# First window steps of the second block written beside the second batch's combine, in shared PSUM pairs and handed-on SBUF places

## The chip, the cores and the metric

The kernel runs on one core of one Trainium2 chip. The metric is device time in microseconds (us) of one execution. Engines are named as in the profile: PE (TensorE), with its weight loads as PEld, DVE (VectorE), ACT (ScalarE), POOL (GpSimd) and SP (SyncE, which here only issues DMAs).

## What is computed

Two batches of 1024 tokens with 256 features pass two blocks. Everything is fp32. Cut to what matters:

```python
x = x + soft_mixture(attention(x))      # block 0
x = x + layers(quaternion_rotation(x))  # block 1, two layers

def soft_mixture(x):                    # 64 experts of 32 slots
    logits = einsum('bmd,dnp->bmnp', x, phi)
    dispatch = softmax(logits, axis=0)                       # over the batch
    combine = softmax(logits.reshape(b, m, n * p), axis=-1)  # over 2048 slots
    slots = einsum('bmd,bmnp->bnpd', x, dispatch)
    y = einsum('bnpd,nde->bnpe', slots, W) + bias
    return einsum('bnpd,bmnp->bmd', y, combine)

def layer(x):
    h = shift_token(x)                  # second half of the features: one token back
    q, k, v = heads(h @ wqkv)           # 8 heads of 64
    q, k = rotary(l2norm(q) * qs, l2norm(k) * ks)
    x = x + local_attention(q, k, v) @ wo   # windows of 128, each sees itself and the one before
    a, g = split(layernorm(shift_token(x)) @ w1 + b1)
    return x + (a * gelu(g)) @ w2 + b2
```

The quaternion rotation is one 256x256 matrix (`rot`), applied to every token.

## The kernel before, in words

Five stages follow each other. **Attention** (lines 140 to 730) works on (batch, group of four heads) units. **The mixture's logits, dispatch and experts** (`logits`, `dispatch`, `experts`, lines 749 to 815) run over 32 iterations `it`: four quarters of the slots, eight pairs of token tiles in each (tile m of both batches). `logits` writes the raw logits to DRAM, one tensor `lgd[i]` of 128 tokens x 2048 slots for each of 16 token tiles; `experts(g0)` makes 8 experts' outputs and adds the bias into `y`. **The combine** (lines 819 to 887) reads those rows back. `weigh(i)` loads row i by one DMA of 1 MB into one of five places, takes its maximum (DVE, line 824), its exp and sum (ACT, 827) and scales it by 1/sum (POOL, 829). `turn(q, jj)` transposes a quarter of the slots of a pair of rows on PE (837) and copies the result from PSUM, on DVE for odd jj (844), on ACT for even (846). `combine(q, jj)` multiplies it with `y` (856); the four quarters of one q gather in one PSUM pair, and the last one adds them to the tokens `xT` on DVE (867). q = 0 to 3 are batch 0, q = 4 to 7 batch 1. `rotate(h)` (879) applies `rot` to half a batch: it fills `xa` through ACT and stores the tokens in DRAM (`xkeep`) for the end. The loop at line 966 writes, for each of 32 parts (q, jj), the turn of the next part and the combine of this one; rotations 0, 1 and 2 stand within it, rotation 3 behind it. Then `psum.close()` gives back all PSUM.

**The window stage** (lines 991 to 1384) covers both layers' attention and feed-forward. Its loop counts steps s from -2 on; window i is 128 tokens, windows 0 to 7 are batch 0 of the first layer, 8 to 15 batch 1. In step s stand the projection and rotation of window s + 2 (`project`, `rotate_parts`, `values`, `norms`, `rotated`), the turn into head-major form of window s + 1, the scores, maxima, exps and divisions of window s in two halves of four heads (`scores` 1122, `maxima` 1139, `weights` 1156, `divide` 1172), the transposed weights of window s - 1 (`turn_e` 1183) and its mix with the values (`mix` 1202). After each fourth window comes `project_out` (1222). The feed-forward follows eight steps later, by `forward(s - 8)`: `centre`, `normalise`, six `gate`s and a `feed` for each 512 tokens, so from s = 6 on.

`rotate_parts` reads the projection's PSUM twice, by ACT (`raw`, 1047) and by DVE (`t1`, 1055); POOL multiplies `raw` with the other table (1057). `norms` is a DVE sum of squares (1066) and twelve small POOL operations (1073 to 1076). The first half of heads is divided on POOL, the second on DVE.

**What sets the order.** Tile makes the semaphores: an instruction waits for the last writers and readers of what it touches. In the window stage PE, DVE, ACT and POOL run in exactly the written order (`manual_schedule`), and each engine's queue is strict: what stands behind a waiting instruction waits too. In the combine's stage only PE's order is written out, and a scheduler orders the rest. SP's order is the scheduler's in both.

**Places.** [...] Before the window stage they are two pools of two pairs (`wide`, `pair`); in it three pairs in a ring (`two_banks`, line 1008) and two single banks (`bank`). A tile in a ring waits for the readers of the tile that held its place. In SBUF the combine's rows, `eT` and `y` lie in pools `mo` and `mo2`; `lw` holds the second block's weights, masks and tables; `la` the window stage's tiles; `fa` the feed-forward's. The weights of the second block's first layer are all loaded before the combine's loop (line 965).

Of the kernel before, what the change touches and what calls it, by code (L numbers as in the profile page):

```python
# [17 lines left out]
P = 128  # L18
# [73 lines left out]
def tile_kernel(ctx: ExitStack, tc: tile.TileContext, a: dict, out: bass.AP):  # L92
# [7 lines left out]
    ones_v = const.tile([P, P], F32, name="ones_v")  # L100
    nc.vector.memset(ones_v, 1.0)
# [22 lines left out]
    wts = ctx.enter_context(ExitStack())  # L124
    with tc.tile_pool(name="xin", bufs=1) as xin, tc.tile_pool(name="l0", bufs=1) as l0, ExitStack() as right:
        xT = xin.tile([P, 2, T], F32, name="xT")

        def load_x(engine, t0, n):
            engine.dma_start(xT[:, :, t0 : t0 + n], a["xT"][:, t0 : t0 + n].rearrange("(c p) t -> p c t", p=P))

        load_x(nc.sync, 0, 512)
        load_x(nc.sync, 512, 512)
        gcoh = l0.tile([P, T // P, H0], F32, name="gcoh")
        fac = l0.tile([P, T // P], F32, name="fac")
# [5 lines left out]
        psum = ExitStack()  # L140
        ps_s = psum.enter_context(tc.tile_pool(name="ps_s", bufs=2, space=PSUM))
        ps_t = psum.enter_context(tc.tile_pool(name="ps_t", bufs=2, space=PSUM))
        at = ExitStack()
        at1 = at.enter_context(tc.tile_pool(name="at", bufs=1))
        at2 = at.enter_context(tc.tile_pool(name="at2", bufs=2))
        w_att = at1.tile([P, 2, N_ATT], F32, name="w_att")
        at0 = {n: W_ATT[n].start for n in W_ATT}
        for engine, lo, n in (
            (nc.scalar, at0["wq"], P),
            (nc.scalar, at0["wk"], P),  # L150
            (nc.scalar, at0["wv"], D),
            (nc.sync, at0["wq"] + P, P),
            (nc.sync, at0["wk"] + P, P),
            (nc.sync, at0["wout"], D),
        ):
            engine.dma_start(
                w_att[:, :, lo : lo + n], a["w_att"][:, lo : lo + n].rearrange("(c p) n -> p c n", p=P)
            )
        mxt = [at1.tile([P, 4, 4, 32], F32, name=f"mxt{i}") for i in range(2)]
        for t in mxt:  # L160
            nc.gpsimd.memset(t, 0.0)

        VW = HD0 + 1
        v = [at1.tile([P, 8, H0 * VW + 32 - VW], F32, name=f"v{b}") for b in range(B)]
        for t in v:
            nc.gpsimd.memset(t, 1.0)
        sv = [at1.tile([P, D], F32, name=f"sv{b}") for b in range(B)]

        def watt(name, c, lo, n):
            at = W_ATT[name].start + lo  # L170
            return w_att[:, c, at : at + n]

        def wide(name):
            return ps_s.tile([P, 2, 512], F32, tag="s", name=name)

        def pair(name):
            return ps_t.tile([P, 2, 512], F32, tag="t", name=name)

        pvs = {}

        def values(b, half, tile, part):

            if part == 0:
                pvs[b, half] = tile("pv").rearrange("p x (y d) -> p (x y) d", d=D)
            pt = pvs[b, half]
            for y in (2 * part, 2 * part + 1):
                j = 4 * half + y
                for k in range(2):
                    nc.tensor.matmul(
                        pt[:, y, :],  # L190
                        xT[:, k, b * S + j * P : b * S + (j + 1) * P],
                        watt("wv", k, 0, D),
                        start=(k == 0),
                        stop=(k == 1),
                    )
            if part == 0:
                return
            nc.vector.tensor_tensor(
                v[b][:, 4 * half : 4 * half + 4, 0 : H0 * VW].rearrange("p j (h d) -> p j h d", d=VW)[
                    :, :, :, 0:HD0  # L200
                ],
                pt.rearrange("p j (h d) -> p j h d", d=HD0),
                bcast(rows[:, ROWS["bv"]].rearrange("p (h d) -> p h d", d=HD0), 1, 4),
                ALU.add,
            )

        def token_sums(b, k):

            if k == 0:
                xws[b] = at2.tile([P, 2], F32, tag="xsum", name="xsum")  # L210
            nc.vector.tensor_reduce(xws[b][:, k : k + 1], xT[:, k, b * S : (b + 1) * S], AX.X, ALU.add)

        def value_sums(b, tile):

            pt = tile("psv")
            for k in range(2):
                nc.tensor.matmul(
                    pt[:, 0, :D],
                    xws[b][:, k : k + 1].to_broadcast([P, P]),
                    watt("wv", k, 0, D),  # L220
                    start=(k == 0),
                    stop=(k == 1),
                )
            nc.vector.scalar_tensor_tensor(
                sv[b], rows[:, ROWS["bv"]], float(S), pt[:, 0, :D], ALU.mult, ALU.add
            )

        units = [(b, g) for b in range(B) for g in range(4)]
        mxs, obs, o_tms, oTs, xws, heads = {}, {}, {}, {}, {}, {}
# [3 lines left out]
        qm = [at1.tile([P, S], F32, name=f"qm{i}") for i in range(2)]  # L233
        qs = [at1.tile([P, S], F32, name=f"qs{i}") for i in range(2)]
        km = [at1.tile([P, S], F32, name=f"km{i}") for i in range(3)]
        for i in (0, 1, 2):
            nc.vector.memset(km[i], 0.0)
            nc.vector.tensor_scalar(km[i], km[i], col("kaug"), None, ALU.add)
            if i < 2:
                nc.vector.memset(qm[i], 0.0)  # L240

        def project_in(b, what, c, tile):

            pt = tile("pqk")
            for n in range(2):
                project_part(pt, b, what, c, n)
            project_end(pt, what, c)

        def project_part(pt, b, what, c, n):
            t0 = b * S + n * 512  # L250
            for k in range(2):
                nc.tensor.matmul(  # L252
                    pt[:, n, :],
                    watt(f"w{what}", k, c * P, P),
                    xT[:, k, t0 : t0 + 512],
                    start=(k == 0),
                    stop=(k == 1),
                )

        def project_end(pt, what, c):  # L260
            heads[what] = at1.tile([P, S], F32, tag=f"h{what}", name=f"h{what}")
            nc.scalar.activation(
                heads[what], pt.rearrange("p n t -> p (n t)"), AF.Identity, bias=col(f"b{what}", c)
            )

        def spread(u):

# [5 lines left out]
        def maxima(step, half):  # L273
# [3 lines left out]
            if hu not in mxs:  # L277
                mxs[hu] = at2.tile([P, 4, 4, 2], F32, tag="mx2", name=f"mx2_{hu}")
# [145 lines left out]
        with tc.tile_pool(name="pro", bufs=1, side="right") as pro:  # L424
# [68 lines left out]
            def coherence_in(b, n, c):  # L493
# [12 lines left out]
                if c == 0:  # L506
                    return
# [995 lines left out]
```

## Time and profile before

| | |
|---|---|
| median of 3 runs | 1725.86 us (1725.84 to 1725.88) |
| the profiled execution | 1725.92 us |
| its span, first to last instruction | 1724.1 us |
| TensorE's clock, mean granted | 0.989 |
| combine, batch 0 / batch 1 | about 804 to 887 / 887 to 967 us |
| window steps s = -2 to 7 | 967 to 1115 us |

The span and 1.8 us around it make the execution. A line of busy time gives the sum of an engine's instructions; matmuls are pipelined and their ends modelled, so two neighbours overlap a little, and the distance of two starts is the better measure of what one costs. The granted clock is a share of full speed. A row of waits names the waiting instruction, what released it, the us in total, how many, and the longest. A stretch's row has one pair of busy time and count for each engine in the order PE, PEld, DVE, ACT, POOL, then the granted clock, the DMA engines' busy share and GB/s.

### The profile page before, as it was taken

To read this page: it belongs to the slowest core of one execution; us is meant where nothing else is said; L and a number is where in the kernel's file an instruction comes from. 1 tells how busy PE (TensorE), PEld (TensorE's weight loads), DVE (VectorE), ACT (ScalarE), POOL (GpSimd) and SP (SyncE) were. 2 spreads that over 40 slices of the span, in tenths; PEclk is the share of its full clock that TensorE was granted. 3 is DMA by queue.
4 is the path that set the end of the run, shared out by engine and by line. 5 is a ranking of instruction groups with operands and counts; after the bars stand their busy time and mean duration, and the time that the engine had idled before them with its cause. 6 is when DMAs were issued, how large, how long until landed. Compare 5 with 4: busy or idle time off the path is not lost.

```text
span 1724.1 us, 22245 instructions
## 1 busy us (share of the span) xinstructions
PE 1670.0 (97%) x8684; PEld 847.2 (49%) x8684; DVE 930.1 (54%) x1599; ACT 834.3 (48%) x1331; POOL 518.4 (30%) x732
## 2 busy tenths in 40 slices
PE   8999999999999999999999878999999999999998
PEld 4333443343433444445788545545555555555543
DVE  5767767766772222233443366666565656575522
ACT  1456556655667222244332254556565656565520
POOL 2101101111110100023563355555464534455301
PEclk9999999999999999999999988999999999999999
DMA  5100000010000434554731000000100000000000
GB/s 148 50 13 13 1 13 13 1 19 7 1 1 13 135 122 134 158 196 156 278 144 65 13 0 1 1 1 0 62 1 13 1 1 34 17 1 25 1 25 36
DMA packets 41881, 82.55 MB, mean 48 GB/s; under 512 B 3708, under 2 KB 24016, under 8 KB 39216
## 3 DMA queue, kind: packets, MB, share of 16 engines
q1 hardware_dynamic: 39232, 75.29, 13.3%
q0 software_dynamic: 1584, 5.29, 1.1%
q8 instruction: 68, 1.11, 0.3%
q10 hardware_dynamic: 960, 0.56, 0.1%
q14 instruction: 37, 0.30, 0.1%
HBM read 55.95 MB, written 20.97 MB: 45 GB/s over the span
## 4 chain that ended last, share of the span: by engine, by line
PE 87%; DVE 4%; POOL 4%; ACT 3%; issue 1%; DMA 1%; DVEq 0%; ACTq 0%; POOLq 0%
PE sc L314 9%; PE pga L1268 8%; PE po L333 7%; PE lg L755 6%; PE cmb L856 6%; PE sl L781 6%; PE pm L282 6%; PE py L1291 5%; PE pq L1033 4%; PE pwo L1222 3%; PE pv L1089 3%; PE sc L1122 3%; PE pe L1183 3%; PE po L1202 3%; ACT e L322 2%; PE pqk L252 2%
## 5 line engine op out<-in xcount | busy, mean ns | idle before, releaser
L289 DVE TENSOR_REDUCE mx<-pm 128x2 f32<-128x1024 f32 x256 | 304.5, 1220 | 86.6 <-PE pm L282 82.6
L322 ACT ACTIVATE e<-sc 128x1024 f32<-128x1024 f32 x256 | 254.0, 1023 | 90.1 <-PE pm L282 49.3
L282 PE MATMUL pm<-km,qm 32*128 32x512 f32 x1024 | 270.3, 633 | 3.3 <-DVE mx L289 2.1
L314 PE MATMUL sc<-qs,km 32*128 32x512 f32 x1024 | 253.5, 612 | 9.0 <-ACT e L322 8.1
L351 POOL TENSOR_TENSOR ob<-ob,part 128x512 f32<-128x512 f32 x43 | 54.6, 1269 | 421.4 <-ACT part L350 421.4
L314 PEld LDWEIGHTS sc<-qs,km 32*128 32x128 f32 x1024 | 85.5, 183 | 134.2 <-ACT e L322 68.0
L1172 POOL TENSOR_SCALAR e<-e,den 128x256 f32<-128x256 f32 (+1 forms) x128 | 129.7, 1026 | 45.7 <-DVE den L1168 45.7
L1268 PE MATMUL pga<-hc,w 128*128 128x512 f32 x320 | 141.1, 593 | 0.0
L1139 DVE CUSTOM_DVE_ANT_0 e<-sc,mask,zn 128x256 f32<-128x256 f32 (+1 forms) x256 | 103.4, 461 | 51.1 <-PE sc L1122 51.1
L1156 ACT ACTIVATE e<-e,nmx 128x256 f32<-128x256 f32 (+1 forms) x256 | 123.5, 486 | 5.5 <-DVE nmx L1139 5.2
L333 PE MATMUL po<-e,v 128*32 128x512 f32 x1024 | 124.8, 605 | 0.7 <-ACT e L322 0.6
L829 POOL TENSOR_SCALAR e<-e,den 128x2048 f32<-128x2048 f32 x16 | 87.0, 5442 | 113.0 <-DVE den L828 84.8
L1033 PE MATMUL pq<-wqkv,xa 128*128 128x512 f32 x256 | 117.4, 602 | 0.0
L755 PE MATMUL lg<-phi,xa 128*128 128x512 f32 x256 | 115.9, 595 | 0.3 <-ACT xa L407 0.3
L856 PE MATMUL cmb<-eT,y 128*128 128x256 f32 x512 | 115.8, 380 | 0.2 <-ACT eT L846 0.2
L1057 POOL TENSOR_TENSOR t<-raw,tabs 128x512 f32<-128x512 f32 x64 | 81.1, 1288 | 114.1 <-ACT raw L1047 112.0
L781 PE MATMUL sl<-dsp,xb 128*128 128x512 f32 x256 | 114.9, 592 | 0.0
L856 PEld LDWEIGHTS cmb<-eT,y 128*128 128x128 f32 x512 | 94.9, 190 | 12.2 <-ACT eT L846 0.5
L765 DVE TENSOR_TENSOR l<-lg,keep 128x512 f32<-128x512 f32 x32 | 22.1, 691 | 135.8 <-ACT keep L763 135.6
L1278 ACT ACTIVATE gl<-pga,cols 128x512 f32<-128x512 f32 (+1 forms) x48 | 33.0, 687 | 124.6 <-PE pga L1268 117.1
L1183 PE MATMUL pe<-ident,e 128*128 128x128 f32 x480 | 73.0, 287 | 20.6 <-POOL e L1172 18.6
L1268 PEld LDWEIGHTS pga<-hc,w 128*128 128x128 f32 x320 | 59.2, 190 | 68.0 <-issue 66.3
(200 smaller groups left out, 2472.9 us busy)
## 6 DMA issues: line engine op xcount, KB each, us to landing
lgd<-keep SPq DMA_DIRECT2D x64, 256.0 KB, 2.4
w<-in_ffn_W SPq DMA_DIRECT2D x16, 1024.0 KB, 7.2
e<-lgd SPq DMA_DIRECT2D x16, 1024.0 KB, 5.6
wqkv<-in_wqkv SPq DMA_DIRECT2D x2, 1536.0 KB, 8.4
w<-in_w SPq DMA_DIRECT2D x2, 1386.0 KB, 10.1
km<-hk SPq DMA_DIRECT2D x32, 64.0 KB, 2.3
qm<-hq SPq DMA_DIRECT2D x32, 64.0 KB, 2.3
phi<-in_phi SPq DMA_DIRECT2D x1, 2048.0 KB, 7.9
```

Source lines behind the costliest of these rows:

```text
L282: nc.tensor.matmul(pm[:, x, :], qm[u % 2][r, i * P : (i + 1) * P], km[u % 3][r, n * 512 : (n + 1) * 512], start=True, stop=True,)
L289: nc.vector.tensor_reduce(mxs[hu][:, i % 4, 2 * half : 2 * half + 2, n], pm, AX.X, ALU.max)
L314: nc.tensor.matmul(sc[:, x, :], km[u % 3][r, j * P : (j + 1) * P], qs[u % 2][r, n * 512 : (n + 1) * 512], start=True, stop=True,)
L322: nc.scalar.activation(e, sc, AF.Exp, scale=1.0 / HD0**0.5)
L333: nc.tensor.matmul(po[32 * hh : 32 * hh + 32, :], v[b][:, j, at : at + 32], es[s + j - j0, hh // 2][:, hh % 2, :], start=(j == j0), stop=( ...
L755: nc.tensor.matmul(lg[:, b, :], xa[:, k, b, 1 + m * P : 1 + (m + 1) * P], phi[:, k, n * 512 : (n + 1) * 512], start=(k == 0), stop=(k == 1),)
L781: nc.tensor.matmul(accs[n][b][:, c, :], xo_tm[:, b * 8 + m, c * P : (c + 1) * P], d[:, b, :], start=(m == 0), stop=(m == 7),)
L856: nc.tensor.matmul(acs[q][:, c, :], y[:, 4 * jj + j, b, c * P : (c + 1) * P], eT[:, j // 2, j % 2 * 256 : (j % 2 + 1) * 256], start=(jj == ...
L1033: nc.tensor.matmul(pq[:, x, :], shifted(xa, k, b, w * WIN, P), load["wqkv"][:, k, x * 512 : (x + 1) * 512], start=(k == 0), stop=(k == 1),)
L1172: engine.tensor_scalar(e[:, x, c, lo:], e[:, x, c, lo:], den[:, x, c : c + 1], None, ALU.mult)
L1183: nc.tensor.transpose(pe[:, j, x, c, :], e[:, x, c, j * WIN : (j + 1) * WIN], ident)
L1268: nc.tensor.matmul(pt[:, x, :], load["w1"][:, k, lo : lo + P], hcs[f][:, k, :], start=(k == 0), stop=(k == 1))
```

## The change

On PE the combine's loop ends with q = 3. The sixteen parts of q = 4 to 7 and rotations 1 to 3 are written into the window loop: three parts in steps -2 and -1, two in 0 to 4, at three points (`a` after the first scores, `c` after the values, `b` after the norms). A table `READY` places the last rows' maximum and exp (`weigh`) and their scaling (`scale`) at such points, in the written order of DVE and ACT. Rotation 3, and the loads of the feed-forward's `w1` and `w2`, stand at the end of s = 5.

What goes with it:
- The window stage's PSUM ring is two pairs (`ps_b`) while parts remain; the third (`ps_c`) is the combine's accumulator, and joins the ring after the last part. `wide` and `pair` are bound to these, so `turn_w` and `rotate` take pairs from the same ring as the projections, scores and transposed weights.
- The rows have four places in one tile (`ebig`) instead of five. A row is fetched in four DMAs of 256 KB; from row 4 on each is issued after the `turn_w` that has read the old row's same quarter. Rows 0 to 3 are weighed from iteration 24 on.
- The scaling is on DVE instead of POOL.
- The transposed quarters go to `xb`'s part for batch 1, which the window stage first writes later.
- `y` and `xT` are two tiles each, one a batch; the experts' bias add is two instructions.
- Places are handed on: `phi` to `wqkv` and `wo`, the logits' `keep`, `l1` and `dsp` to `raw`, `mask` and `tabs` (in two halves), `ebig` to the feed-forward's `u`, `w2`, `yo`, `rs`, `sq` and `gl` (parts of one tile), `y1` to `w1`, `xT[0]` to `oT`, `xT[1]` to `hc`. The experts' weights move from the right side of SBUF to the left, over attention's tiles.
- An unused tile of ones and its memset go.

The diff's core, without the lines that only change their indentation:

```diff
-            nc.vector.tensor_tensor(
-                y[:, g0 : g0 + 2, :, :], py, bcast(ybs[g0 // 4][:, i : i + 2, :], 2, B), ALU.add
-            )
+        for b in range(B):
+            nc.vector.tensor_tensor(y[b][:, g0 : g0 + 2, :], py[:, :, b, :], ybs[g0 // 4][:, i : i + 2, :], ALU.add)
...
+    def row(i):
+        return ebig[:, i % 4, :]
+
+    def fetch(i, jj):
+        at = slice(jj * 512, (jj + 1) * 512)
+        nc.sync.dma_start(row(i)[:, at], lgd[i][:, at])
 
         def weigh(i):
-            e = mo2.tile([P, NS], F32, tag="e", name="e", bufs=5)
-            nc.sync.dma_start(e, lgd[i])
...
-            nc.vector.tensor_reduce(nmx, e, AX.X, ALU.max)
+        nc.vector.tensor_reduce(nmx, row(i), AX.X, ALU.max)
...
-            nc.scalar.activation(e, e, AF.Exp, bias=nmx, accum_out=den)
+        nc.scalar.activation(row(i), row(i), AF.Exp, bias=nmx, accum_out=den)
+        dens[i] = den
+
+    def scale(i):
+        den = dens.pop(i)
             nc.vector.reciprocal(den, den)
-            nc.gpsimd.tensor_scalar(e, e, den, None, ALU.mult)
-            wes[i] = e
+        nc.vector.tensor_scalar(row(i), row(i), den, None, ALU.mult)
 
-        def turn(q, jj):
+    def turn_w(q, jj):
...
-            eT = mo2.tile([P, 2, 512], F32, tag="eT", name="eT", bufs=2)
+        wTs[q, jj] = xb[:, jj % 2, 1, 1 : 1 + S].rearrange("p (x n) -> p x n", x=2)
...
+        for i in (2 * q + 4, 2 * q + 5):
+            if i < T // P:
+                fetch(i, jj)
...
+    xp = ctx.enter_context(tc.tile_pool(name="xp", bufs=1, side="right"))
+    ebig = xp.tile([P, 4, NS], F32, tag="e", name="ebig")
...
+    dx = dxs.enter_context(tc.tile_pool(name="dx", bufs=2))
...
-                if it >= ITS - 6 and it % 2 == 0:
-                    weigh((it - ITS + 6) // 2)
-            weigh(3)
-            weigh(4)
+            if it >= ITS - 8 and it % 2 == 0:
+                i = (it - ITS + 8) // 2
+                for jj in range(4):
+                    fetch(i, jj)
+                weigh(i)
+                scale(i)
...
-            weights2(0, "wqkv", "tabs", "wo", "w1", "w2")
-            for q in range(8):
+        weights2(0, "wqkv", "tabs", "wo")
+        for q in range(4):
                 for jj in range(4):
+                if jj == 0:
+                    for i in (2 * q + 2, 2 * q + 3):
+                        if 4 <= i:
+                            weigh(i)
+                            scale(i)
                     if q == 0 and jj < 3:
                         continue
...
-            rotate(3)
...
+    ps_b = ctx.enter_context(tc.tile_pool(name="ps_b", bufs=2, space=PSUM, reuse_waits="tile"))
+    ps_c = ctx.enter_context(tc.tile_pool(name="ps_c", bufs=1, space=PSUM, reuse_waits="tile"))
...
+        def third(name):
+            return ps_c.tile([P, 2, 512], F32, tag="c", name=name)
+
+        mixing, ring = [None], []
+
         def two_banks(name):
-            return ps_b.tile([P, 2, 512], F32, tag="b", name=name)
+
+            if not mixing:
+                ring.append(name)
+            return third(name) if len(ring) % 3 == 1 else ps_b.tile([P, 2, 512], F32, tag="b", name=name)
+
+        wide, pair = two_banks, third
...
+        mixing = [(q, jj) for q in range(4, 8) for jj in range(4)]
+        PARTS = {-2: "acb", -1: "acb", 0: "ab", 1: "ab", 2: "ab", 3: "ab", 4: "ab"}
+        READY = {
+            (-2, "a"): ((weigh, 10),),
+            (-2, "c"): ((scale, 10), (weigh, 11)),
+            (-2, "b"): ((scale, 11),),
+            (-1, "b"): ((weigh, 12),),
+            (0, "a"): ((scale, 12), (weigh, 13)),
+            (0, "c"): ((scale, 13),),
+            (1, "b"): ((weigh, 14),),
+            (2, "a"): ((scale, 14), (weigh, 15)),
+            (2, "c"): ((scale, 15),),
+        }
+
+        def beside(s, point):
+            if point in PARTS.get(s, ""):
+                if len(mixing) > 1:
+                    turn_w(*mixing[1])
+                q, jj = mixing[0]
+                combine(q, jj)
+                mixing.pop(0)
+                if (q, jj) in ((4, 1), (6, 1)):
+                    rotate(q // 2 - 1)
+            for f, i in READY.get((s, point), ()):
+                f(i)
...
             if now:
                 scores(s, 0)
+            beside(s, "a")
             if before:
                 turn_e(s - 1, 0)
...
                 keep_values(s + 2)
+            beside(s, "c")
             if now:
                 scores(s, 1)
...
                 norms(s + 2)
+            beside(s, "b")
             if 0 <= s - 2 < WINDOWS and (s - 2) % 4 == 3:
                 project_out((s - 2) // 4)
...
+            if s == 5:
+
+                rotate(3)
+                f = xp.tile([P, 4 * NS], F32, tag="e", name="f")
...
+                fa["hc"] = xin.tile([P, 2, 2, 512], F32, tag="x1", name="hc")
+                load["w2"] = fa["w2"]
+                load["w1"] = xp.tile([P, NE // 4 * D], F32, tag="y1", name="w1")[:, : 2 * W1N].rearrange(
+                    "p (k n) -> p k n", k=2
+                )
+                weights2(0, "w1", "w2")
```

## The prediction

> **What bounds the kernel now.** I read the page's shares and slices first, then busy time by stretches cut at the window steps, then TensorE's waits, then one step of each engine's timeline.
>
> ```profile
> span 1724.1 us, 22245 instructions
> PE 1670.0 (97%) x8684; PEld 847.2 (49%) x8684; DVE 930.1 (54%) x1599; ACT 834.3 (48%) x1331; POOL 518.4 (30%) x732
> ...
> PE   8999999999999999999999878999999999999998
> ...
> PEclk9999999999999999999999988999999999999999
> ```
> TensorE is busy 97%; moving work can pay only where it is idle or slow, and that is slices 22 to 24, some 948 to 1077 us.
>
> ```profile
> 861.10:887.10 26.00, 26.00 (x147) 23.23 (x146) 12.27 (x14) 8.74 (x9) 16.79 (x4) 1.00 0.42 162
> 887.10:966.60 79.50, 78.99 (x402) 65.52 (x401) 22.66 (x31) 18.98 (x19) 27.18 (x5) 1.00 0.19 67
> 966.60:971.70 5.10, 5.10 (x13) 2.26 (x12) 0.45 (x1) 2.47 (x3) 0.40 (x1) 1.00 0.00 0
> 971.70:980.90 9.20, 6.31 (x22) 3.13 (x21) 5.72 (x7) 3.63 (x5) 7.89 (x16) 1.00 0.00 0
> 980.90:991.50 10.60, 9.52 (x38) 4.46 (x36) 7.14 (x16) 3.90 (x8) 6.93 (x15) 0.84 0.01 3
> 991.50:1008.50 17.00, 12.92 (x54) 6.47 (x54) 10.04 (x37) 9.26 (x28) 9.11 (x18) 0.80 0.00 0
> 1008.50:1026.70 18.20, 14.22 (x79) 8.21 (x77) 11.01 (x30) 9.46 (x23) 10.23 (x18) 0.91 0.00 1
> 1026.70:1043.90 17.20, 14.56 (x86) 8.72 (x85) 10.67 (x30) 8.94 (x23) 10.18 (x18) 0.90 0.00 0
> 1043.90:1061.10 17.20, 14.57 (x87) 8.82 (x86) 10.76 (x30) 9.03 (x23) 10.18 (x18) 0.90 0.00 1
> 1061.10:1085.10 24.00, 21.36 (x103) 11.75 (x102) 11.89 (x33) 11.28 (x31) 12.77 (x30) 0.93 0.00 1
> ```
> Columns: the stretch, its length, then busy us of PE, PEld, DVE, ACT, POOL, then granted clock. The second row is the whole combine of batch 1 with three rotations: PE full, other engines a quarter to a third (PEld apart). Rows three to nine are steps s = -2 to 4, the tenth is s = 5. There PE is idle 17.3 us in s = -2 to 4, at a clock down to 0.80.
>
> ```profile
> PE pe L1183 <- POOL e L1172: 17.3, 21, 3.5
> PE pt L1107 <- DVE t L1083: 2.9, 1, 2.9
> ```
> The wait that ends last is for POOL's division. The chain of waits in a step runs: scores, maxima on DVE (4 x 0.41), sum of squares (1.2), 12 small POOL operations (3.6 to 4.5), four divisions (4.2), transposition. It is latency, not throughput: there is room for PE work beside it.
>
> **What PE needs in these steps.** At full clock, by starts in PE's timeline from 1085 us on: projection 3.45, values 1.72, scores 1.07 a half, transposed weights 0.87 a half, mix 1.03 (two halves, 2 x 0.5 in window 0), turn 0.87, output projection 6.88. Summed in program order, s = -2 to 4 need 5.2 + 6.0 + 7.3 + 9.5 + 11.4 + 11.9 + 11.9 = 63.4, and they take 1061.1 - 966.6 = 94.5. So 31.1 us are idle or slow clock. That is the room.
>
> **What is moved.** Sixteen parts, each 0.87 (turn) + 3.46 (combine) = 4.33, and rotations of 3.43. The new stage starts where combine (3,3) ends, 887.1, because the b = 0 part keeps its order on PE. PE's need per step, with three parts in s = -2 and -1, two in 0 to 4, rotation 1 in s = -2 and 2 in s = 1: 21.6, 19.0, 16.0, 21.6, 20.1, 20.6, 19.7 (no turn in the last part); sum 138.6. With no stall s = 5 would start at 1025.7 instead of 1061.1.
>
> **What the moved step puts on the other queues.** DVE, ACT and POOL run in written order here. DVE gets half the copies (1.22 each), the adds (0.74 a quarter), reductions (2.29 + 0.14) and the scaling that POOL did. ACT gets the other copies (1.01), exps (2.0 + 0.19), two rotation copies. POOL loses 16 x 5.44 = 87 us, on which nobody waited, so that is worth 0.
>
> The scaling on DVE is a new form: 128x2048, SBUF to SBUF. Row by row DVE's L1172 has 281 ns at best and 436 mean for 256 elements; extended by its mean slope against the 128-element form (288 ns) that is 436 + 1792 x 1.16 = 2.5 us. L238, the same form at 1024, took 0.62, 0.86 and 1.17. The Trainium skill, "VectorE: DVE Perf Modes", section on the perf-mode tier table, says that such an fp32 operation runs at two elements a cycle, 1227 ns for 2048. The best rows (281 at 256, 625 at 1024) extend to 1.1, and the slow ones lie beside busy POOL, which is idle at most of the new places. I take 1.2, plus 0.16 for the reciprocal; with 2.5 the stage below is 3 us longer.
>
> Stalls follow from order and from two PSUM pairs where there were three: a tile waits for the reader two tiles before.
> - s = 0: the first turn waits for the raw copy and rotation product of the projection (1.0 + 1.2 after it ends, minus 0.64 of scores): 1.6. The second scores wait for maxima, which stand behind copy, scaling and a 2.4 reduction: 1.0. Scaling 13 then waits on DVE for its exp; maxima queue behind it, and the next turn for them: 2.0. Sum 4.6.
> - s = 2: the same reduction and scaling sit ahead of maxima: from scores' end 0.75 + 0.87 + 1.22 + 1.3 + 2.4 + 1.65 = 8.2, against 5.1 of PE work and stall before the transposition that needs the pair: 3.15. With 0.6 behind the rotation's copy (ACT) and 0.75 as in the next point: 4.5.
> - s = 1, 3, 4: DVE copies the transposed weights (1.22), then does two rotation products (1.85), the divide (1.8) and the next product (1.2), 6.1 in all, against 5.55 of PE: 0.55 a step. s = 1 has 1.2 for want of a mix, and 0.5 for ACT's late copy; s = 4 has 0.8 for the last adds, as the accumulator's pair returns to the ring. Sum 1.7 + 0.7 + 1.5.
>
> Together 13.0; stage 138.6 + 13.0 = 151.6, s = 5 at 1038.7: 22.4 earlier. POOL's chain (about 12.6 from scores to division's end) now has 17 us of PE work beside it, so its 17.3 us of waits go; DVE's order is next.
>
> s = 5 takes rotation 3 (3.43) but its 18.9 of need no longer meets the wait: 22.3 against 24.0, gain 1.7. s = 6 and after I leave as they are.
>
> **Clock, against the change.** The Trainium skill, "TensorE: Matmul & The Clock Gate", Part 1, says PE falls to half clock after an idle window of about 3.4 us; by that my largest stall, 3.15, costs nothing more. The trace is harsher: after 2.89 us of waiting at 977.5 the next projection took 5.30 us instead of 3.60. I take the row: 1.7, once, in s = 2. Handoffs between engines, 0.05 to 0.1 at some 13 stalls: 1.
>
> **The rest.**
> - Rows come as 64 pieces of 256 KB instead of 16 of 1 MB, each queued on SP behind its turn; behind it stand weights, kept tokens and later pieces. An issue is 0.32 us (21 in all), SP has room; landing is 2.4 to 3.4 (the row that writes lgd), against 5.6. From turn (q,3) to turn (q+2,0) PE has 20.8 us; needed 0.7 + 3.4 + two reductions 4.9 + exp 2.2 + scaling 1.4 + DVE's other copies and adds 3.2 = 15.8. Slack 5 hides it; a DVE order that waits for an exp ahead of a copy would cost up to 3 for each of three row pairs. Not below 0, as PE waits for no row now. I take 0.5.
> - Expert weights now lie where attention's tiles were, so their first load waits for the end of attention; first use is six iterations of 6.9 us later. Cover enough; without it one 7.4 us load.
> - w1 and w2 load at s = 5 instead of some 230 us earlier: 14.1 and 15.5 us to landing in the trace, first use in s = 8, 50 us on. Hidden by steps 5 to 7; without cover some 10.
> - Second-layer weights overwrite the same tile, tables come in two halves, u, gl, sq and others share one tile: 0 if waits follow the part that is touched (PE was busy 250.0 of 250.0 us from 1150 to 1400, so there is no gain); if whole tiles were waited for, about one load's landing, 8 us.
> - Output bias in two adds of 0.69 instead of one of 1.22: 8 x 0.16 on DVE beside full PE; one memset of 0.165 gone: 0.
>
> **Sum.** 22.4 + 1.7 - 1.7 - 1.0 - 0.5 = 20.9. The profiled execution was 1725.92 (span 1724.1 and 1.8 around it), 0.06 from the median of 1725.86. So 1725.9 - 20.9 = 1705.0.
>
> **Rivals.**
> - Filled nearly whole: stalls melt into each other. The bound is 31.1 + 3.43 + 0.9 of moved ends, + 1.7 in s = 5: gain 37, 1689; say 1689 to 1696. For it: the other engines' busy time in s = 3 and 4 is about 11 + 2 of 21. Against: the order with reductions ahead of maxima. 0.13.
> - Rows late, or more order stalls (DVE and ACT waiting on each other in s = -2 and -1 too): 6 to 16 us lost again, 1711 to 1721. For it: four row places instead of five, and DVE does what POOL did. 0.19.
> - It doesn't do what it says: a reused place or pair makes the first projections wait for the end of the combine; nothing overlaps, 1724 to 1728. Against: those places' last readers, by program order, are done by 887. 0.04.
> - Slower: the clock. The moved matmuls leave a place where PE ran at 1.00 for one with 0.80 to 0.93. If stalls keep the gate closing, 138.6 + 22.3 = 160.9 us of need run at 0.80 (s = 1 now): 201 us even with all stalls hidden in it, against 198.0 now from 887.1 to 1085.1, so 1729, and up to 1740 with stalls on top. It decides below a mean clock of 0.81, or 0.88 if my 16 us of stalls come on top. Against: PE is busy nine tenths of this stage. 0.06.
> The case I forecast, 1697 to 1713, has 0.58.
>
> **How the numbers follow.** 1705 is that case. 1692 to 1717 takes in most of the second case and part of the first, and leaves out about 0.2. A measurement of this kernel tells 0.2% (3.5 us) from no change: faster 0.90, same 0.04, slower 0.06.
>
> **What would show it.** Right: from about 887 PE's rows alternate cmb with pq and sc; s = 5 starts near 1039; waits of pe for POOL's division nearly gone there, waits for DVE's maxima and rotation product in their place, 1 to 3 us each, mostly in s = 0 and 2; clock above 0.95; DVE's scaling near 1.2 us; PE unbroken before 887. Wrong: PE waiting for DVE's scaling or a DMA of rows before 887, gates in s = 8 waiting for w1, a mean clock under 0.9 in the stage, or scaling of 2.5 us.

## The result and the profile after

The changed kernel takes 1709.79 us (median of 4 runs, 1709.11 to 1710.98), beside 1725.87 for the kernel before (1725.84 to 1727.93): ratio 0.9905, 95% interval 0.9887 to 0.9922. That is 16.1 us gained, where 20.9 was predicted. In all tables and texts below, a span is that of one profiled execution.

The page's shares and slices of the kernel after:

```profile
span 1708.3 us, 22359 instructions
PE 1659.0 (97%) x8684; PEld 842.9 (49%) x8684; DVE 950.6 (56%) x1622; ACT 830.1 (49%) x1329; POOL 426.2 (25%) x716
...
PE   8999999999999999999999899999999999999998
...
PEclk9999999999999999999999999999999999999999
```
The dip of three slices has shrunk to one, slice 22 (940 to 982 us), and the 8s in the row of the clock are gone. DVE has 20 us more than before, POOL 92 less: the scaling has moved.

Busy time by stretches, cut where the projection of each step starts (s = -2 to 5; columns as before):

```profile
889.89:911.47 21.58, 21.58 (x93) 15.37 (x92) 13.02 (x16) 8.56 (x9) 5.09 (x14) 1.00 0.31 98
911.47:930.49 19.02, 19.02 (x94) 14.74 (x93) 11.16 (x14) 7.49 (x8) 6.11 (x14) 1.00 0.27 83
930.49:953.48 22.99, 18.32 (x85) 12.98 (x84) 11.25 (x27) 9.52 (x23) 5.09 (x14) 0.93 0.08 24
953.48:978.16 24.68, 22.47 (x109) 14.71 (x107) 13.95 (x35) 10.04 (x24) 8.65 (x18) 1.00 0.06 22
978.16:1000.99 22.83, 21.01 (x124) 15.10 (x125) 16.88 (x38) 13.70 (x27) 9.64 (x18) 1.00 0.00 1
1000.99:1022.86 21.87, 20.99 (x135) 15.45 (x133) 12.28 (x31) 9.87 (x23) 9.53 (x18) 1.00 0.01 1
1022.86:1044.91 22.05, 20.32 (x126) 14.49 (x125) 12.96 (x32) 8.97 (x22) 9.54 (x18) 1.00 0.20 60
1044.91:1067.75 22.84, 22.78 (x110) 12.23 (x109) 14.98 (x34) 8.98 (x22) 11.03 (x19) 1.00 0.24 82
```
The first two steps are full at 21.58 and 19.02 us, the 21.6 and 19.0 of the forecast: there PE's need is all. From s = 0 on each step is 1 to 7 us longer than its need (16.0, 21.6, 20.1, 20.6, 19.7), and only s = 0 ran at a reduced clock.

TensorE's waits inside the stage (889 to 1068 us):

```profile
PE pe L844 <- DVE t L1083: 5.7, 5, 1.8
PE pe L844 <- DVE nmx L1167: 2.8, 2, 2.6
PE pe L1211 <- DVE xT L876: 0.8, 1, 0.8
PE pq L1061 <- ACT xa L892: 0.7, 1, 0.7
PE sc L1150 <- DVE nmx L1167: 0.7, 1, 0.7
```
L844 is the turn of the next part. It now waits for a pair that DVE has not yet read: for the rotation product (`t1`, L1083), once a step, and for the maxima (L1167), of which one wait is long. POOL's division, 17.3 us before, is no longer among these rows; 2.5 us of it are left in the whole kernel, in later steps.

Where the 15.8 us between the spans lie is read from the starts of the same step in both traces:

| point | before | after | gain so far |
|---|---|---|---|
| s = 5 | 1061.1 | 1044.9 | 16.2 |
| s = 6 | 1085.1 | 1067.8 | 17.3 |
| s = 8 | 1115.2 | 1097.3 | 17.9 |
| s = 9 | 1136.1 | 1119.4 | 16.7 |
| last projection | 1576.0 | 1561.6 | 14.4 |
| end | 1724.1 | 1708.3 | 15.8 |

So 17.9 was gained up to s = 8, late start included, and 3.5 went again between s = 8 and the last projection.

### The profile page after: what moved, and what is told of

Read it like the earlier page. It is cut to its first block, busy times and chain, and to the rows that moved or that the text cites. A ratio compares the mean times of both kernels' runs of the same rounds, so it can differ in the third digit from the quotient of the medians.

```text
span 1708.3 us, 22359 instructions
## 1 busy us (share of the span) xinstructions
PE 1659.0 (97%) x8684; PEld 842.9 (49%) x8684; DVE 950.6 (56%) x1622; ACT 830.1 (49%) x1329; POOL 426.2 (25%) x716
## 4 chain that ended last, share of the span: by engine, by line
PE 86%; DVE 7%; ACT 4%; POOL 1%; issue 1%; DMA 1%; DVEq 0%; ACTq 0%; POOLq 0%
PE sc L314 9%; PE pga L1296 8%; PE po L333 7%; PE lg L754 7%; PE sl L780 6%; PE pm L282 6%; PE cmb L865 6%; PE py L1319 5%; PE pq L1061 4%; PE pwo L1250 3%; PE sc L1150 3%; PE pe L1211 3%; PE po L1230 3%; PE pv L1117 2%; ACT e L322 2%; PE pqk L252 2%
## 5 line engine op out<-in xcount | busy, mean ns | idle before, releaser
L1167 DVE CUSTOM_DVE_ANT_0 e<-sc,mask,zn 128x256 f32<-128x256 f32 (+1 forms) x256 | 103.5, 462 | 45.4 <-PE sc L1150 45.4
L780 PE MATMUL sl<-dsp,xb 128*128 128x512 f32 x256 | 116.7, 600 | 2.0 <-ACT dsp L769 2.0
L865 PE MATMUL cmb<-xb,y 128*128 128x256 f32 x512 | 117.6, 383 | 0.2 <-ACT xb L853 0.2
L1061 PE MATMUL pq<-wqo,xa 128*128 128x512 f32 x256 | 115.7, 595 | 0.7 <-ACT xa L892 0.7
L865 PEld LDWEIGHTS cmb<-xb,y 128*128 128x128 f32 x512 | 95.8, 192 | 12.8 <-ACT xb L853 0.5
L1075 ACT COPY raw<-pq 128x1024 f32<-128x1024 f32 x32 | 32.4, 1012 | 134.7 <-PE pq L1061 134.7
L1306 ACT ACTIVATE f<-pga,cols 128x512 f32<-128x512 f32 (+1 forms) x48 | 32.9, 686 | 125.8 <-PE pga L1296 118.4
L282 PEld LDWEIGHTS pm<-km,qm 32*128 32x128 f32 x1024 | 77.2, 183 | 28.7 <-DVE mx L289 14.8
```

Of the source, the lines that this page charges most:

```text
L282: nc.tensor.matmul(pm[:, x, :], qm[u % 2][r, i * P : (i + 1) * P], km[u % 3][r, n * 512 : (n + 1) * 512], start=True, stop=True,)
L780: nc.tensor.matmul(accs[n][b][:, c, :], xo_tm[:, b * 8 + m, c * P : (c + 1) * P], d[:, b, :], start=(m == 0), stop=(m == 7),)
L865: nc.tensor.matmul(acs[q][:, c, :], y[b][:, 4 * jj + j, c * P : (c + 1) * P], eT[:, j // 2, j % 2 * 256 : (j % 2 + 1) * 256], start=(jj == ...
L1061: nc.tensor.matmul(pq[:, x, :], shifted(xa, k, b, w * WIN, P), load["wqkv"][:, k, x * 512 : (x + 1) * 512], start=(k == 0), stop=(k == 1),)
```

## The experiments

My theory: the overlap itself gives what PE's need says, and three things take some of it back. (1) Row work on DVE and ACT (a reduction 2.28, an exp 2.0, a scaling 1.29) stands in the written order ahead of maxima and rotation products for which a turn waits. (2) Rows weighed from iteration 24 on delay a dispatch, so that the stage starts late. (3) The ring of fixed pairs costs later steps some 2 us. The rivals: the moved matmuls gain less because the shared pairs as such are too few; the late start comes from late transfers; the later loss comes from something else than the ring.

Each ratio is to the kernel before on the same chip; its medians there lie between 1725.2 and 1725.9, so the medians of different rows can be compared to within 0.7 us.

| kernel | us | ratio to before, 95% interval | span |
|---|---|---|---|
| after | 1709.79 | 0.9905 [0.9887, 0.9922] | 1708.3 |
| parts first | 1747.04 | 1.0128 [1.0115, 1.0141] | 1747.1 |
| parts first, row work spread | 1732.73 | 1.0047 [1.0033, 1.0060] | 1730.1 |
| rows earlier | 1713.29 | 0.9935 [0.9923, 0.9947] | 1711.2 |
| combine and maxima first | 1709.95 | 0.9917 [0.9904, 0.9931] | 1708.1 |
| both | 1706.44 | 0.9891 [0.9878, 0.9904] | 1705.8 |
| POOL scales the stage's rows | 1721.22 | 0.9973 [0.9964, 0.9983] | 1720.2 |
| POOL scales the earlier rows | 1707.79 | 0.9896 [0.9883, 0.9910] | 1706.2 |
| before, with a fixed ring | 1727.69 | 1.0011 [1.0005, 1.0018] | 1725.3 |
| rows weighed later | 1707.71 | 0.9897 [0.9882, 0.9912] | 1705.5 |
| best order | 1699.18 | 0.9847 [0.9833, 0.9860] | 1697.2 |

### Parts first

All sixteen parts and rotation 3 stand ahead of the steps again, in the new places and pairs.

```diff
+        for q in range(4, 8):
+            for jj in range(4):
+                if jj == 0 and q < 7:
+                    for f in (weigh, scale):
+                        for i in (2 * q + 2, 2 * q + 3):
+                            f(i)
+                if len(mixing) > 1:
+                    turn_w(*mixing[1])
+                combine(q, jj)
...
+        rotate(3)
+        PARTS, READY = {}, {}
```

> Placement alone undone: all sixteen parts and the rotations stand ahead of step -2, everything else of the change stays. Theory (the gain is the 31 us of waits and slow clock of the steps being filled, nothing else of the change helps): the gain is gone and the change's costs remain, 2.8 us ahead of the combine's second half and about 2 us after step 8, so 1728 to 1732 us, with POOL's division as the largest wait again (17 us) and the clock at 0.8 to 0.93 in the steps. Rival (places, POOL's relief, split loads or fewer waits bring part of the gain): under 1724.

It took 1747.04, some 15 us above this: a miss. The order of my own edit was the cause. From DVE's timeline, and then PE's, of this kernel (start, us, engine, line, operation; in brackets the idle time before it and what ended it):

```profile
917.11 1.28 DVE L837 TENSOR_SCALAR ebig<-ebig,den 128x2048 f32<-128x2048 f32 x1
919.17 0.17 DVE L836 RECIPROCAL den<-den 128x1 f32<-128x1 f32 x1 [0.77 <-ACT ebig L831]
919.37 1.29 DVE L837 TENSOR_SCALAR ebig<-ebig,den 128x2048 f32<-128x2048 f32 x1
920.57 1.22 DVE L851 COPY xb<-pe 128x1024 f32<-128x1024 f32 x1
```
```profile
921.84 5.41 PE L865 MATMUL cmb<-xb,y 128*128 128x256 f32 x16 [5.00 <-DVE xb L851]
```
Two reductions, two exps and two scalings, written in one place, kept the copy of the transposed weights back, and PE idled 5.00 us, twice; the matmuls after it took 5.41 and 5.22 instead of 3.62. That is 13.4 us, and it is point (1) at its plainest.

### Parts first, row work spread

The same, with at most one reduction between two parts:

```diff
+                i = 2 * q + 2
+                if q < 7 and jj < 3:
+                    for f, n in (((weigh, i),), ((weigh, i + 1), (scale, i)), ((scale, i + 1),))[jj]:
+                        f(n)
```

> All sixteen parts and the last rotation ahead of the steps again, but with the rows' reductions, exponentials and scalings one at a time between the parts, so that no copy of transposed weights stands on VectorE behind a scaling that waits for an exponential. In the first trial of parts first, the combine lost 10.0 us in two waits of 5.0 for such copies and 3.2 in slow matmuls after them. Theory: those 13 us were the trial's own order, so this takes 1732 to 1736: the kernel before, plus 3.4 for the rotation that no longer lies in window 5's wait, plus about 2.3 for the shared pair of the later steps and 2 to 3 in step 8. The overlap is then worth 22 to 27 us against the kernel after. Rival: parts first is itself dear in the new places (four row places, copies into the shared tile): still 1742 to 1748.

1732.73, within the theory's range; the rival falls. The two waits of 5.00 are gone. Against the kernel before, the first step starts 3.1 later (1.9 of it comes from ahead of the combine's second half, 1.2 from within), s = -2 to 5 are 0.8 shorter, s = 8 is 2.8 longer, the later steps 2.3, the tail 1.4 shorter: 6.0 in sum, the difference of the spans. So the overlap alone is worth 23 us (1732.7 against 1709.8; by the ratios 24.5), and what comes with it costs 6 to 8. One term of the expectation was wrong, and the range was met in spite of it: the 3.4 for rotation 3. In the kernel before, too, that rotation stands ahead of the steps (at 963.0), and s = 5 takes 24.0 us without it in both.

### Rows earlier

Rows 12 and 13 are weighed and scaled at the end of s = -1, rows 14 and 15 weighed at the end of s = 0 and scaled at the end of s = 1.

```diff
-            (-1, "b"): ((weigh, 12),),
-            (0, "a"): ((scale, 12), (weigh, 13)),
-            (0, "c"): ((scale, 13),),
-            (1, "b"): ((weigh, 14),),
-            (2, "a"): ((scale, 14), (weigh, 15)),
-            (2, "c"): ((scale, 15),),
+            (-1, "b"): ((weigh, 12), (weigh, 13), (scale, 12), (scale, 13)),
+            (0, "b"): ((weigh, 14), (weigh, 15)),
+            (1, "b"): ((scale, 14), (scale, 15)),
```

> Only the last rows' maxima and scaling are moved: weigh 12, 13 and scale 12, 13 to step -1 point b, weigh 14, 15 to step 0 point b, scale 14, 15 to step 1 point b, where DVE waits for POOL's norms. Theory (reductions and scaling ahead of the maxima in DVE's queue cause the waits of 0.35 and 2.56 in s = 0 and 0.65 in s = 2, and the 2.56 brings the slow clock that costs 1.6 more): step 0 shrinks from 23.0 to about 18.5, step 2 by 0.6, total 1704 to 1706. Rival (two PSUM pairs cause those waits whatever DVE does): they stay, 1709 to 1710.

1713.29, a miss with the wrong sign: slower than the kernel after. Its waits in the stage:

```profile
PE pe L844 <- DVE t L1083: 11.6, 5, 5.5
```
The wait for maxima went, but the row work met the next product in the order: two exps on ACT stood ahead of the copy `raw`, two reductions on DVE ahead of `t1`, and the turn waited 3.54 in s = 0 and 5.52 in s = 1. "Earlier" was the wrong cure; the stall goes to whatever comes next on the queue.

### Combine and maxima first

In a step the part's combine comes ahead of the next turn, and the first half's maxima stand on DVE ahead of the turn's copy.

```diff
                 q, jj = mixing[0]
                 combine(q, jj)
+                if point == "a" and s >= 0:
+                    maxima(s, 0)
+                if len(mixing) > 1:
+                    turn_w(*mixing[1])
```

> In each part the combine now stands before the next turn on PE, and at point a of steps 0 to 4 the first half's maxima stand on DVE before the turn's copy, rows' scaling and reductions. Theory (turns at point a wait for the rotation product's release of a PSUM pair, 1.77, 1.35, 0.77, 0.88, 0.88 us in s = 0 to 4): 3.46 us of combine cover these five, 5.7 us go, and the maxima no longer stand behind reductions; perhaps 1 us a step comes back as the transposed weights wait for the later copy: 1703 to 1707. Rival (DVE's round from transposed weights to rotation product sets the step, so that a wait only moves): 1708 to 1711.

1709.95: no gain by the medians, the rival's figure. Steps 0, 1, 3 and 4 became 3.5, 1.0, 0.4 and 0.8 us shorter, but s = 2 took 27.2 instead of 22.8. PE's timeline, then ACT's, of this kernel:

```profile
992.20 1.68 PE L1230 MATMUL po<-eT,v 128*64 128x128 f32 x16 [4.46 <-ACT eT L1217]
```
```profile
989.16 2.00 ACT L831 ACTIVATE ebig<-ebig,nmx 128x2048 f32<-128x2048 f32 x1 [8.58 <-DVE nmx L829]
991.07 0.19 ACT L831 ACTIVATION_READ_ACCUMULATOR ebig<-ebig,nmx 128x1 f32 x1
991.16 0.99 ACT L1217 COPY eT<-pe 128x1024 f32<-128x1024 f32 x1
```
ACT stood idle 8.58 us at the exp of row 15, which waited for the row's maximum on DVE, and behind it stood the copy for which PE waited.

### Both

The two edits together.

> Both of the two edits before. Theory: their gains add except where they remove the same wait (the maxima behind reductions): 1700 to 1704, clock near 1.0 through the stage, steps 0 to 4 within 1 us of PE's need of 16.0, 21.6, 20.1, 20.6, 19.7. Rival: no better than the better one of the two.

1706.44, some 2 us above the range expected, but better than either edit alone: the two orders take each other's stall away. Left over in s = 0 and s = 1 are waits of 3.13 and 0.98 for `t1`.

### POOL scales the stage's rows

```diff
-        nc.vector.tensor_scalar(row(i), row(i), den, None, ALU.mult)
+        (nc.gpsimd if i >= 10 else nc.vector).tensor_scalar(row(i), row(i), den, None, ALU.mult)
```

> Of the change only this is undone: rows 10 to 15 are scaled on POOL (5.44 us each) instead of DVE, at the same written points. Theory (POOL's place in the steps is free, but its queue is strict, so a scaling of 5.4 ahead of norms and division, twice in s = 0 and twice in s = 2, is late for the turn that needs the row): 4 to 9 us slower than the change, 1714 to 1719, waits of turns for POOL in s = 0 and 2. Rival (DVE is the crowded engine, so taking 1.5 us off it four times outweighs): 1705 to 1709.

1721.22, dearer than expected. The kernel's waits in the stage:

```profile
PE pe L844 <- POOL ebig L837: 11.4, 4, 4.9
PE pe L844 <- DVE t L1083: 5.8, 5, 1.7
```
On POOL one scaling takes 5.44 us, and the turn waits for it: 11.4 us in four waits. From the start of the stage to s = 5 this kernel takes 11.8 us longer than the kernel after. The waits for `t1` stay, so they do not hang on DVE's scaling; the wait for maxima went from 2.8 to 0.2, so that one did. The scaling on DVE was thus a needed part of the change, not a detail.

### POOL scales the earlier rows

The same line with `i < 10`, so that rows 0 to 9 are scaled on POOL, as before.

> Rows 0 to 9 scaled on POOL as before, the steps' rows on DVE. It asks for the cause of the 2.05 us wait of a dispatch for its sigmoid near 780 us and the 1.8 us of slow clock behind it. If the scaling on DVE causes it (1.44 us ahead of the subtraction): the wait shrinks below 0.8 and the slow matmuls go, 1706 to 1708. If the order of a row's exp and a table load ahead of the sigmoid on ACT causes it, which the scheduler makes: the wait stays or moves, 1709 to 1711.

1707.79, two below the kernel after; the intervals overlap, so the trace has to speak. PE's timeline of the kernel after, then of this one, at the same dispatch:

```profile
780.49 5.40 PE L780 MATMUL sl<-dsp,xb 128*128 128x512 f32 x8 [2.05 <-ACT dsp L769]
```
```profile
779.33 3.70 PE L780 MATMUL sl<-dsp,xb 128*128 128x512 f32 x8
```
The wait of 2.05 and the slow matmuls behind it are gone, and the stage starts at 887.7 instead of 889.9. What stood ahead of that dispatch in the kernel after is seen in its timelines of DVE, then of ACT:

```profile
773.89 2.29 DVE L828 TENSOR_REDUCE nmx<-ebig 128x1 f32<-128x2048 f32 x1 [1.33 <-DMA ebig<-lgd]
...
776.47 1.29 DVE L837 TENSOR_SCALAR ebig<-ebig,den 128x2048 f32<-128x2048 f32 x1
777.67 0.68 DVE L764 TENSOR_TENSOR l<-lg,keep 128x512 f32<-128x512 f32 x1
```
```profile
776.40 2.00 ACT L831 ACTIVATE ebig<-ebig,nmx 128x2048 f32<-128x2048 f32 x1 [1.24 <-DVE nmx L829]
778.31 0.19 ACT L831 ACTIVATION_READ_ACCUMULATOR ebig<-ebig,nmx 128x1 f32 x1
778.51 1.28 ACT L769 ACT_TABLE_LOAD   x1
779.80 0.63 ACT L769 ACTIVATE dsp<-l 128x512 f32<-128x512 f32 x1
```
The scheduler put the exp of the fourth row and a table load of 1.28 ahead of the dispatch's activation. Its input `l` was done at 778.35, so DVE's scaling was not what it waited for. With scalings on POOL the scheduler orders this otherwise, and the fourth exp comes after it (781.11). The rival of late transfers falls too: the fourth row's reduction waited 1.33 us for its DMA above, but with scalings on POOL it began later still, at 775.73 after 6.79 us of waiting for its DMA, and PE lost nothing. So what was gained is an order, not the 1.29 us themselves.

### Before, with a fixed ring

The kernel before, with its three pairs taken in turn from two pools, so that every third tile has the same place:

```diff
+            ring.append(name)
+            if len(ring) % 3 == 1:
+                return ps_c.tile([P, 2, 512], F32, tag="c", name=name)
             return ps_b.tile([P, 2, 512], F32, tag="b", name=name)
```

> The kernel before with one edit: the window stage's three PSUM pairs are one fixed ring of a pool of one and a pool of two, as the change has after the last part, instead of one pool of three. If the fixed ring is what costs 2 us after step 8 (second scores waiting for the rotation product, 0.57 four times, and a slow clock once): 1726.5 to 1729. If those come from the change's other parts: 1725.5 to 1726.3.

1.9 us more by the medians (ratio 1.0011, interval above 1). From step 9 on TensorE has a wait that the kernel before does not have, scores for `t1`, 1.8 us in three waits here. In the kernel after it is this row:

```profile
PE sc L1150 <- DVE t L1083: 2.3, 4, 0.6
```
Between s = 9 and the last projection it loses 1.9 on the kernel before; the kernel after loses 2.3 there. So point (3) holds for the later steps. For s = 8 the ring gives 0.6 of the 1.2 us.

### Rows weighed later

Rows 0 to 2 are weighed two iterations later, row 3 after the last dispatch.

```diff
-            if it >= ITS - 8 and it % 2 == 0:
-                i = (it - ITS + 8) // 2
+            for i in (it - ITS + 6,):
+                if i < 0 or i % 2:
+                    continue
+                i //= 2
```

> The change with rows 0 to 2 weighed at iterations 26, 28 and 30 and row 3 after the loop, as before, instead of 24 to 30. If two reductions at once near 772 us come from the earlier written places: the 2.05 us wait of the dispatch goes, 1706 to 1708. If the scheduler's order makes it in any case: 1709 to 1711, or a wait of a like size elsewhere.

1707.71, but not for the reason given: the dispatch still waited, 1.84 instead of 2.05. The matmuls after it ran at full speed (3.70), and the stage started 1.2 earlier. So the wait does not hang on how early rows are asked for, but on where the scheduler puts the exp, and that the range was met is luck. The other 1.6 us of the span lie in the tail: there this execution has no stretch at half clock, where the kernel after has one (shown under "s = 6 and after" below).

### Best order

Combine and maxima first, the earlier rows scaled by POOL, and row work where each queue has room:

```diff
-            (-1, "b"): ((weigh, 12), (weigh, 13), (scale, 12), (scale, 13)),
+            (-1, "b"): ((weigh, 12), (weigh, 13)),
+            (0, "a"): ((scale, 12), (scale, 13)),
             (0, "b"): ((weigh, 14), (weigh, 15)),
             (1, "b"): ((scale, 14), (scale, 15)),
```

> Combine ahead of the turn with the maxima ahead of the copy of transposed weights, the rows weighed early, rows 12 and 13 scaled only after window 0's first maxima, and the rows before 10 scaled by GpSimd. Theory (VectorE's and ScalarE's written order makes the stage's stalls, row work in front of maxima and rotation products being the cause): 1705.8 of span in the trial with both orders, less 2.2 for the stage's earlier start, less 2 to 3 of the 3.1 us that window 0 waited for its rotation product: 1699 to 1703. Rival: the waits move to the next product in line, as in the two single orders: 1704 to 1708.

1699.18 (1698.52 to 1699.24): 26 us below before and 10.6 below after, within the theory's range; the rival falls. s = 0 in this kernel's stretches:

```profile
929.06:945.39 16.33, 16.33 (x86) 11.73 (x85) 13.31 (x32) 11.76 (x25) 3.61 (x8) 1.00 0.22 65
```
PE is full for 16.33 us, at full clock, against a need of 16.0 in the prediction and 22.99 in the kernel after. It has the same two pairs, places and engines. So the pairs as such were not too few in that step: the stall was the order on DVE and ACT. Of the 11.1 us between its span and that of the kernel after, 2.1 lie ahead of the stage, as with POOL's scaling of the earlier rows alone, and 8.8 in the stage. 6.7 of these are s = 0, whose waits (4.7) and stretch at half clock (1.7) are gone. s = 1 still takes 24.89, 3.3 over its need.

## Why the prediction was nearly right, point by point

- **PE's need and the start.** Right in size: s = -2 and -1 took 21.58 and 19.02, s = 0 in the best order 16.33. The stage from its start to s = 5 took 155.0 against 154.3 (138.6 need, 13.0 stalls, 1.7 clock, 1.0 handoffs). That this sum came so near is in part luck: s = 0, 1, 3 and 4 are 2.4, 1.4, 0.6 and 0.8 longer than forecast, and s = 2, with the fall of the clock that was expected in it, is 3.5 shorter. (The needs of the kernel before add up to 63.2, not 63.4; nothing hangs on it.)
- **Start at 887.1: the step that failed most.** The text said that the part for batch 0 keeps its order on PE, and "I take 0.5" for rows. PE's order was kept; ACT's was not. The stage started at 889.9, 2.8 late, and 2.2 of that went when POOL scaled the early rows. The sign named for it ("PE unbroken before 887") was the right one to watch; its price was set too low, because only the fetches and the slack inside the combine were costed, not the row work between dispatches.
- **Stalls of s = 0.** 4.6 were predicted. The waits were 1.77 for `t1` (1.6 predicted), 0.35 for the transposition's pair (1.0, then for the second scores) and 2.56 for maxima behind scaling 13 (2.0): 4.7. Right by place and by size.
- **s = 1, 3 and 4.** The waits for `t1` came, 1.35, 0.88 and 0.88; the steps are 3.1, 1.3 and 2.35 over their need, where 1.7, 0.7 and 1.5 were predicted.
- **s = 2.** The stall of 3.15 did not come: the step waited 0.77, 0.65 and 0.66 in its larger waits and took 22.83 instead of 26.3. The chain itself was as long as said: the first half's maxima ended 8.5 after the scores, where 8.2 was predicted. Wrong was which tile waits for them. The transposition started at 988.67 without a wait; the second scores, which stand 2.6 of PE work later (0.87 transposition, 1.72 values), waited 0.65.
- **Clock.** In the stage the size was right and the place wrong: one group of slow matmuls, 5.17 instead of 3.63, after 2.56 us in s = 0. Between 100 and 1600 us the kernel after runs three times at half clock, each time for 3.41 us: at the dispatch ahead of the stage, after 2.05, which was not foreseen, then in s = 0 and in s = 8:
```profile
780.94:784.35 3.41, 3.41 (x5) 1.35 (x4) 1.29 (x2) 1.64 (x4) 0.00 (x0) 0.50 0.41 154
948.19:951.60 3.41, 3.41 (x11) 2.79 (x10) 0.65 (x3) 1.93 (x7) 1.94 (x9) 0.50 0.00 0
1105.20:1108.61 3.41, 3.41 (x8) 1.40 (x6) 3.38 (x7) 1.01 (x1) 2.64 (x3) 0.50 0.02 5
```
Half of 3.41 is 1.7 us of work lost in each. That clocks fell after waits shorter than the 3.4 us of the Trainium skill's page "TensorE: Matmul & The Clock Gate", Part 1, was what the prediction had chosen by the row.
- **Scaling on DVE.** 1.29 against the 1.2 taken and the 1227 ns of "VectorE: DVE Perf Modes", perf-mode tier table. The 2.5 of the row's slope is out.
- **s = 5.** 22.84 instead of 22.3: a gain of 1.1, not 1.7.
- **s = 6 and after, left at 0.** 0.5 gained in s = 6, 1.2 lost in s = 8, 2.3 lost to the last projection, 1.4 gained behind it. The middle two come to 3.5, more than the late start. The fixed ring explains about 2.5 of it. In s = 8 the values' matmuls took 3.39 instead of 1.88, at half clock, after the same waits of 0.18, 0.57 and 0.57 as before. That cost nothing: in "combine and maxima first" they ran at full speed, and the scores behind them waited for `t1` instead:
```profile
1108.21 0.71 PE L1150 MATMUL sc<-qkT 64*128 64x128 f32 x8 [1.76 <-DVE t L1083]
```
The step took 22.08 there and 22.09 in the kernel after, so `t1` sets its length. The shorter tail is the clock and no merit of the change. In the kernel before, the kernel after and "rows weighed later", in this order, the 20 us around the same wait of 1.27 us are:
```profile
1619.65:1639.65 20.00, 17.53 (x67) 8.45 (x64) 10.74 (x25) 6.52 (x19) 7.67 (x8) 0.83 0.00 1
1605.19:1625.19 20.00, 17.27 (x69) 8.17 (x66) 10.74 (x25) 6.52 (x19) 7.64 (x8) 0.91 0.01 1
1604.11:1624.11 20.00, 17.27 (x86) 8.48 (x82) 11.46 (x27) 6.53 (x19) 7.66 (x8) 1.00 0.00 1
```
The clock is 0.83, 0.91 and 1.00, and the way from the last projection to the end 148.1, 146.7 and 145.0 us.
- **Loads.** No gate waited for `w1` or `w2`, as predicted; no PE wait in the stage names a row's DMA.

From the forecast 20.9, in order: -2.8 start, -0.7 stage, +0.5 rows, -0.55 s = 5, +0.5 s = 6, -1.2 s = 8, -2.3 later, +1.4 tail give 15.75, the 15.8 between the spans. The case forecast, 1697 to 1713, held; without the 1.4 of the tail and the 3.5 of s = 2, an estimate from these figures, the kernel would have taken 1714.7 and lain outside it. The slower rival's mechanism was real in single waits but never near deciding: the mean clock in the stage's worst step was 0.93, and 0.994 in the whole kernel.

## What to carry to other kernels

Work that moves beside a latency-bound stage can fill most of its idle time (some 23 of 31 us here), and then the in-order queues of the *other* engines set the rest: for each long operation that is written between short ones, ask which copy stands behind it and who waits for that copy. Moving it to an earlier place only hands the stall to the next in line; of the two single edits here one lost 3.5 us and the other gained nothing, while the order that gave each queue its room gained 10.6, some 2 of it ahead of the stage. And follow what comes with an edit (where rows are scaled, how tiles take their places) outside the stage too: most of the shortfall lay before and behind it.

## What the runs showed of the hardware

- The same eight matmuls (`sl`, L780) took 3.70 us after waits of 1.42, 1.43, 1.72, 1.74 and 1.84 us, and 5.40 after 2.02, 2.05 and 2.17, in eight kernels. Length alone does not decide elsewhere: 2.55 and 2.56 before L844 brought 5.10 to 5.30 for the following combine, while after 2.98 in "combine and maxima first" the turn and the projection ran at full speed (1.09 and 3.60). Nor do the waits alone decide in the tail, where the same instructions wait 1.27, 0.23 and 0.29 us: the kernel before ran 6.83 us at half clock there, the kernel after 3.41, "rows weighed later" none. A window of activity that runs free of the program, as the Trainium skill's "TensorE: Matmul & The Clock Gate", Part 1, has it, would let the same wait fall well or badly, and the stretches at half clock are as long as the window given there, about 3.4 us; but all these waits are shorter than such a window. How much idle time within one is enough was not measured.
- A small POOL operation that begins beside a DVE product of two SBUF operands ends only with it. In the kernel after, DVE and then POOL:
```profile
927.18 1.22 DVE L1110 TENSOR_TENSOR t<-t,t 128x1024 f32<-128x1024 f32 x1
```
```profile
927.25 1.22 POOL L1101 TENSOR_TENSOR nt<-zn 128x16 f32<-128x16 f32 x1
```
All 19 of the `norms` operations on POOL that began beside this product took 1.12 to 1.23 us. The 72 that began beside the copy `eT`, which reads PSUM, took 0.20 to 0.22, and so did the 16 beside a row's reduction, which has one operand. In the kernel before it is 25 operations, of 1.06 to 1.19 us: one such operation among the twelve of `norms` adds 0.9, the difference between the 3.6 and the 4.5 us of the prediction's chain. The Trainium skill's "GPSIMD Engine Reference", section 8, says that POOL shares its SBUF interfaces with DVE and contends with instructions that have two SBUF inputs; these rows agree.
